# A two-layer graph network in fp32: idle products and late work at the joint, transposes in two items, pairs made one ahead, and less background in one panel's scores

## The chip, the cores and the metric

The kernel runs on one core of one Trainium2 chip. The metric is the device time of one execution in microseconds (us); less is better. A program on one core has its matmuls on TensorE (PE), its vector work on VectorE (DVE), activations and copies on ScalarE (ACT), a little vector work and the stores on GpSimd (POOL), and the loads are issued by SyncE (SP). The numbers are from the profiler's record of one execution and from the times of three runs.

## The reference

There are N = 2708 nodes with D = 1024 features, all in fp32, and a 0/1 matrix `adj` of N x N. Each of two layers normalizes its input, forms attention scores, masks them with `adj`, and adds the attended features to its input:

```python
# layer 0
h = relu(layernorm(x));  f = h @ Wf;  g = h @ Wg
e = relu(f @ g.T)
attention = softmax(where(adj > 0, e, -9e15), axis=1)
x = x + attention @ (h @ W0)
# layer 1
h = relu(layernorm(x)) @ W1
e = leaky_relu((h @ a1) + (h @ a2).T, 0.2)
attention = softmax(where(adj > 0, e, -9e15), axis=1)
x = x + relu(attention @ h)
```

(The biases are zero in this case, and are left out here.)

## The kernel before, in words

**Tiles and stages.** The nodes form tiles of 128 rows. Two tiles make a pair; there are ten pairs (`NQ`), and a last unit `LEFT` that holds what is left over: the tile `MONO` and a small one, `TINY`. The columns of the attention matrix are worked through in five panels of 576, 576, 532, 512 and 512. Large matrix products go by Strassen's scheme: seven products M1 to M7 on halves in place of eight, with sums of blocks made ahead by DVE.

The order of the stages is: M = Wg Wf' in 256 products into `M_ps` (L593), up to about 147 us; `project_q` of panel 0, to 206; then for each panel p its scores (L1409), a softmax, the aggregation and the projection by W; the projection of the next panel's q lies in between. Scores of panel 0 take 206 to 365, those of panel 3 1408 to 1541. Layer 0 ends at about 2036 to 2099 with the last panel's projection and the joint, where the first exponents of layer 1 are made; layer 1 begins with `gx` (L685) at 2099.

**Scores.** `scores` runs over the ten pairs q. For each it makes the seven products M1, M6, M5, M2, M7, M3 and M4 of 8 matmuls (1.94 us apiece in panel 0, 13.58 us for an iteration; 1.73 in panel 3). The left operand `As` of a product comes from `hs_d[q]` in DRAM, in four loads for each pair, each of two products. `hs_d[q]` holds seven transposed blocks of pair q, which `make_pairs` has made and stored. After each product DVE adds it to `m1`, `t` (`st`), `sa` or `sb`, and then `behind(rate)` lets background work run. The last product of a pair, M4, is run after M1 of the next one.

**Background.** `later` is a list of pieces of work. Each has a price in us, a fetch and a body. `behind(us)` (L207) adds `us` to a credit, bounded by twice that, and runs pieces from the list's head as long as the credit is positive. So `rate` sets how much background follows each product. `make_until(q)` (L547) runs the list's head, without regard to credit, until pair q is made. A piece's fetch is issued a few pieces ahead (`ahead`). Inside scores `nc.hold = ("vector",)` keeps DVE's instructions in the order in which they are written. SP's loads are always in written order; a load into a stream buffer waits until the buffer's last reader or store is done, and every load behind it waits too.

**make_pairs** (L434) puts for each pair, in the order 0, 1, LEFT, 2, ... 9: the two normalizations of the next pair (`put_norms`), its rows, its transposes, `dots` (two dot products with a bias vector, for pairs 0 and 1 later on) and `last`: the sums on DVE and the four stores of `hs_d[q]` by POOL. `transposes(q)` (L464) turns both tiles of a pair: 4 x 4 transposes on PE into four PSUM banks `h_ps` (L457), from which ACT copies to `hsT`; for panel 0's tiles DVE copies a part of them too. This is one piece with the price 0.5, and it takes PSUM banks. In the stage of M such a piece runs between the products.

In scores, the pairs that aren't made yet are made ahead of their use: `make_until(q + 2)` stands at each iteration's head (L1458), and the rate is 1.3 until pair 9 is made, then `rates[p]`, which is 0.8, 1.0, 0.65, 0.65 and 0.65 for the five panels (L1419).

At the end of panel 0's rows a small column `r_d` per panel is stored by POOL (L275), 512 elements of 4 bytes.

**The joint.** `rows_done` (L1587) is called with each tile of layer 0's output. For the tiles of the last panel it works directly and not through `later`. The last tile of pair 9 (`ends`) closes layer 0. `keep_on(t, n)` (L1580) issues n products whose result nobody reads, of the identity with a row tile t (`on_ps`): three on `xt[0]` (tile `x_res`) ahead of the tile's normalization, two on the normalized rows (`h_last`). Then come the dots, `raise_max` (the maximum `mx` over masked scores' terms), and `shifts1`, which turns mx over the partitions (`mx_ps`, L894), reduces it (`mcol`), and from it works out `m`, `z` and `none`; in between (`keep_on(mx[0], 1)` and `make()`) one more idle product and the first part of `pair_h` (L355), which makes sums of row blocks of h for layer 1. `pair_h` gives back its second part, `rest()`: two subtractions on DVE (`g`, 128 x 512) and the stores of the blocks M3 and M7 into `hr_d`. `rest[0]()` is called right there, held in written order.

Afterwards `weights1` (L1834) spreads shift, z and none over the partitions (`sp_ps`, L265), subtracts the shift from the first, already prepared tiles (`P`), starts the exponents, and puts pieces of 2.1 into a list `front`, which goes to the head of `later`.

Of the kernel before, what the change touches and what calls it, by code (L numbers as in the profile page):

```python
# [18 lines left out]
P = 128  # L19
# [38 lines left out]
def kernel(  # L58
# [22 lines left out]
    NH = NC // 2  # L81
# [28 lines left out]
    NQ = len(pairs)  # L110
    pair_of = {t: (t // 2, t % 2) for t in range(MONO)}
    LEFT = NQ
# [328 lines left out]
    def make_pairs():  # L441
        xs, hT = {}, {}

        def fetch(q):
            xs[q] = []
            for t in units[q]:
                xs[q].append(row_halves("x"))
                load_rows_of(t, xs[q][-1], x)

        def rows(q):  # L450
            left_h(0, *xs[q]) if q == LEFT else rows_h(q, *xs[q])

        def turned(q, k, e):
            t = units[q][k]
            ps = bank("h_ps", (P, NH, P))
            for c in range(NH):
                nc.tensor.transpose(ps[:, c, :], xs[q][k][e][:, c * P:(c + 1) * P], ident)  # L457
            for i, (s, n) in enumerate(pieces[0]):
                if s == t:
                    o = first_h[e].rearrange("p (c i) -> p c i", c=NH)[:, :, i * P:i * P + n]  # L460
                    nc.vector.tensor_copy(o, ps[:, :, :n])
            return ps

        def transposes(q):  # L464
            if q == LEFT:
                two = stream("hsl", (P, 2, NH, P))
                for e in range(2):
                    nc.scalar.copy(two[:, e], turned(q, 0, e))
                    nc.scalar.copy(tinyT[:, e], turned(q, 1, e)[:, :, :B32])
                store(hsl_d.rearrange("p e c j -> p (e c j)"), two.rearrange("p e c j -> p (e c j)"))  # L470
            else:
                ts = [stream("hsT", (P, 2, NH, P)) for _ in range(4)]
                hT[q] = ts, lambda i: ts[i // 2][:, i % 2]
                for k, e, i in ((0, 0, 0), (0, 1, 3), (1, 0, 7), (1, 1, 6)):
                    nc.scalar.copy(hT[q][1](i), turned(q, k, e))
            turned_tiles.update(units[q])

        def sums(q):
            if q == LEFT:
                return  # L480
            ts, i = hT.pop(q)
            at = {m: i(k) for k, m in enumerate(BY_SCORES)}
            add(at[M5], i(7), at[M4])
            sub(at[M6], at[M5], at[M1])
            sub(at[M7], at[M1], i(7))
            sub(at[M3], at[M2], at[M6])
            for g, t in enumerate(ts):
                store(hs_d[q][:, 2 * g:2 * g + 2].rearrange("p m c j -> p (m c j)"), t.rearrange("p m c j -> p (m c j)"))

        def dots(q, k):  # L490
            t = units[q][k]
            c = col_of[t]
            dot(r_[:, c:c + 1], xs[q][k], [vb[e][:, :W] for e in range(2)], c0)
            if t == MONO:
                nc.gpsimd.dma_start(r_[:NM, HALF:HALF + 1], r_[NM:, c:c + 1])

        def drop(q, what):
            seen.setdefault(q, set()).add(what)
            if len(seen[q]) == 3:
                xs.pop(q)  # L500

        def last(q):
            sums(q)
            drop(q, "sums")
            made.add(q)

        def bias(q, k):
            dots(q, k)
            drop(q, f"dots{k}")

        seen = {}
        def put_norms(q):
            put(2.1, lambda: normalize(xs[q][0]), lambda: fetch(q))
            put(2.1, lambda: normalize(xs[q][1]))

        put_rows = lambda q: put(0.5, lambda: rows(q))
        def put_dots(q):
            for k in range(2):
                put(1.6, lambda k=k: bias(q, k), ready=lambda: vb[0] is not None)

        todo = [0, 1, LEFT] + list(range(2, NQ))
        put_norms(todo[0])
        for i, q in enumerate(todo):
            if i + 1 < len(todo):
                put_norms(todo[i + 1])
            put_rows(q)
            put(0.5, lambda q=q: transposes(q), takes_psum=True)
            if 1 < i < 4:
                put_dots(q)
            put(2.7 if q != LEFT else 0.0, lambda q=q: last(q))  # L530
            if i >= 4:
                put_dots(q)
            if i == 1:
                put_dots(todo[0])
                put_dots(todo[1])
# [870 lines left out]
    def scores(p, B):  # L1406
# [9 lines left out]
            row_on_all(rb, r_d[p], p)  # L1416
        acc = slot("acc")
        S = [None] * NT
        rates = (0.8, 1.0, 0.65, 0.65, 0.65)  # L1419
        lefts = {}  # L1420

        def product(q, m, ps, start):
# [32 lines left out]
        left_over = None  # L1455
        for q in range(NQ):
            n = P
            make_until(q + 2)  # L1458
            rate = 1.3 if NQ - 1 not in made else rates[p]
            if q + 3 <= LEFT:  # L1460
                fetch(q + 3)
            if p == 0 and q == NQ - 2:
                ahead[0] = 2
                sums_h()
            if p in ORDERED and q in (2, 6):
                (copy_residual if q == 2 else bias_residual)(p)
            sa, sb = slot("Sa"), slot("Sb")
            S[pairs[q][0]], S[pairs[q][1]] = sa, sb
            X, Y, Z = (bank(f"s{k}") for k in "xyz")
            m1, t = slot("sm1"), slot("st")  # L1470
            product(q, M1, X, True)
            for s in (lo, hi):
                add(m1[:n, s], X[:n, :h], rb[:n, s])
            if left_over:
                left_over()
            product(q, M6, Z, True)
            add(t[:n, lo], Z[:n, :h], m1[:n, hi])
            behind(rate, True)
            product(q, M5, Y, True)
            add(t[:n, hi], Y[:n, :h], m1[:n, hi])  # L1480
            if q + 2 <= LEFT:
                convert(q + 2, p > 0)
            behind(rate, True)
            product(q, M2, X, False)
            add(sa[:n, lo], X[:n, :h], rb[:n, lo])
            if q + 2 <= LEFT:
                turn(q + 2, 0)
            behind(rate, True)
            product(q, M7, Z, False)
            add(sb[:n, hi], Z[:n, :h], t[:n, hi])  # L1490
            if q + 2 <= LEFT:
                turn(q + 2, 1)
            behind(rate, True)
            product(q, M3, Y, False)
            add(sa[:n, hi], Y[:n, :h], t[:n, lo])
            finish(q, sa, 0)
            behind(2 * rate, True)
            left_over = lambda q=q, sb=sb, Z=Z, m1=m1: last(q, sb, Z, m1)
# [88 lines left out]
    def rows_done(t, xt, fetch=None):  # L1587
# [14 lines left out]
        if panel_of[t] == NP - 1:  # L1602
            done_rows[t] = row_halves("h_last")
            ends = q == NQ - 1 and whole
            if ends:
                keep_on(xt[0], 3)
            normalize(xt, done_rows[t])
            if ends:
                keep_on(done_rows[t][1], 2)
            if whole and q == NQ - 1:  # L1610
                tc.keep_in_program_order(nc.scalar.activation(stats.tile([P, 1], FP, name="warm"), eps, AF.Exp))
            raise_it = lambda: raise_max(0, q, k, first_mask[t][:, :width[0]])
            if not whole:
                dots(1)
                raise_later.append(raise_it)
                dots0 = lambda: dots(0)
                if q == NQ - 1:
                    put(1.6, lambda: held(dots0))
                else:
                    dots0()  # L1620
            else:
                last = q == NQ - 1
                raise_later.pop()()
                dots(1)
                (held if last else call)(raise_it)
                if last:
                    put(1.6, lambda: held(dots, 0))
                else:
                    dots(0)
                rest = []  # L1630
                make = lambda: rest.append(pair_h(q, *(done_rows[s] for s in pairs[q])))
                if last:
                    got["zm"] = held(shifts1, 0, lambda: (keep_on(mx[0], 1), make()))
                else:
                    make()
                (held if last else call)(rest[0])
                put_max(1, q)
                if q == NQ - 1:
                    for m in BY_QUARTERS:
                        put_quarters(m, q // 2, later)  # L1640
                    for p in range(2, NP):
                        for s in (NQ - 2, NQ - 1):
                            put_max(p, s, lazy)
# [182 lines left out]
    def weights1(p, z, m, shift):  # L1826
# [46 lines left out]
        for i in range(len(order) + LAG):  # L1873
            mk = []
            front.append([2.1, (lambda i=i, mk=mk: mk.append(load_mask(p, *order[i])))
                          if i < len(order) and not (p == 0 and units[order[i][0]][order[i][1]] in before) else None,
                          (lambda i=i, mk=mk: go(i, mk)), False, None])
        later[:0] = front
        return S, sm

# [89 lines left out]
```

## Time and profile before

| what | us |
|---|---|
| median of 3 runs | 3032.05 (3030.42 to 3034.79) |
| the profiled execution | 3029.47 |
| its span, first to last instruction | 3027.6 |
| PE busy | 2990.7 (99% of the span) |
| DVE busy | 2052.1 (68%) |
| ACT / POOL busy | 533.6 (18%) / 496.4 (16%) |
| scores of panel 0, first matmul to last | 206 to 365 |
| scores of panel 3 | 1408 to 1541 |
| last projection of layer 0 and joint | 2036 to 2099 |

A busy share is the time in which an engine executes, its own instructions overlapping counted once. A line of the timeline gives start, duration, engine, line of the kernel, operation, output and inputs, shape and count; in brackets stands the idle time ahead of it and who ended it. A line of the waits gives total, times and the longest in us. The table by stretches of time gives for each its length, for each engine its busy time and number of instructions, and then the clock that TensorE was granted (1.00 is full speed), the share of the DMA engines and GB/s.

### The profile page before, as it was taken

Reading aid. Unit: us, or ns where it says so; the run is one execution under the profiler, and the core shown is the slowest. Engines: PE = TensorE matmul, PEld = TensorE weight load, DVE = VectorE, ACT = ScalarE, POOL = GpSimd, SP = SyncE. Lnnn points to the kernel's source line nnn. Section 1 sums busy time; section 2 is a strip of 40 time slices with the busy share of each in tenths; the row PEclk is TensorE's granted clock in tenths of the full one; section 3 lists DMA queues with packets and bytes.
Section 4 is the critical chain, followed back from the end, with each engine's and each line's share of the span. In section 5 each row is a group of like instructions: output and inputs, shape, how many; then the busy total and the mean of one; then the engine's idle time right before and its main releaser. Section 6 shows DMA issues by size and latency. Waiting matters only on the chain.

```text
span 3027.6 us, 41695 instructions
## 1 busy us (share of the span) xinstructions
PE 2990.7 (99%) x14642; PEld 2293.6 (76%) x14642; DVE 2052.1 (68%) x4670; ACT 533.6 (18%) x878; POOL 496.4 (16%) x770
## 2 busy tenths in 40 slices
PE   8999999999999999999999999999999999999999
PEld 5577777667877588876888886885767959879695
DVE  5777794545772566837974366768888768787863
ACT  4420020020210112101220111202231221212200
POOL 1421111200032100233011111131211010020201
PEclk9999999999999999999999999999999999999999
DMA  7989978887388775788957597688768768888887
GB/s 244 293 304 263 324 268 317 248 260 223 117 302 223 226 215 174 263 247 275 287 171 253 179 256 240 233 309 311 261 199 267 265 208 296 287 271 297 262 298 268
DMA packets 395008, 772.11 MB, mean 255 GB/s; under 512 B 65985, under 2 KB 208225, under 8 KB 394769
## 3 DMA queue, kind: packets, MB, share of 16 engines
q1 hardware_dynamic: 334640, 590.13, 60.1%
q0 software_dynamic: 54464, 164.78, 16.1%
q10 hardware_dynamic: 5696, 14.55, 1.4%
q8 instruction: 116, 1.90, 0.2%
q14 instruction: 92, 0.75, 0.1%
HBM read 635.37 MB, written 138.11 MB: 255 GB/s over the span
## 4 chain that ended last, share of the span: by engine, by line
PE 76%; DVE 11%; issue 6%; DMA 4%; ACT 1%; POOL 1%; SPq 1%; POOLq 0%; DVEq 0%; ACTq 0%
PE sz L1431 7%; PE gy L685 6%; PE gz L685 5%; PE gz L1120 5%; PE sx L1431 5%; PE gx L685 5%; PE sy L1431 5%; PE pz L1320 5%; PE py L1320 4%; PE px L1320 4%; PE M_ps L593 3%; PE gx L1120 3%; PE gy L1120 3%; PE gv L685 3%; PE qz L685 3%
## 5 line engine op out<-in xcount | busy, mean ns | idle before, releaser
L1431 PE MATMUL sz<-B,As 128*128 128x288 f32 (+2 forms) x1200 | 291.3, 392 | 2.2 <-DVE st L45 2.0
L1431 PEld LDWEIGHTS sz<-B,As 128*128 128x128 f32 x1200 | 227.7, 190 | 49.3 <-DVE st L45 3.2
L1431 PE MATMUL sy<-B,As 128*128 128x288 f32 (+2 forms) x800 | 200.6, 394 | 2.3 <-DVE acc L45 2.3
L1431 PE MATMUL sx<-B,As 128*128 128x288 f32 (+2 forms) x800 | 199.1, 392 | 2.1 <-DMA As<-hs_d 2.1
L685 PE MATMUL gz<-Sa,hc 128*128 128x288 f32 (+2 forms) x800 | 185.8, 392 | 0.0
L1431 PEld LDWEIGHTS sy<-B,As 128*128 128x128 f32 x800 | 152.9, 191 | 33.4 <-DVE acc L45 2.5
L1431 PEld LDWEIGHTS sx<-B,As 128*128 128x128 f32 x800 | 151.8, 190 | 34.1 <-issue 4.0
L685 PEld LDWEIGHTS gz<-Sa,hc 128*128 128x128 f32 x800 | 151.5, 190 | 32.2 <-issue 2.2
L1120 PE MATMUL gz<-quarter,hc 128*128 128x128 f32 (+2 forms) x1344 | 168.8, 279 | 3.8 <-DVE gT L45 3.7
L1120 PEld LDWEIGHTS gz<-quarter,hc 128*128 128x128 f32 x1344 | 160.6, 191 | 5.1 <-DVE gT L45 4.6
L143 POOL DMA_DIRECT2D out_dram<-x_res x164 | 80.9, 500 | 468.7 <-DVE x_res L45 459.1
L1320 PE MATMUL py<-w,ps 128*128 128x512 f32 x320 | 142.3, 593 | 0.6 <-DMA w<-in_L_gnn_W_dram 0.6
L1320 PE MATMUL pz<-w,ps 128*128 128x512 f32 x320 | 142.0, 594 | 0.0
L1320 PE MATMUL px<-w,gT 128*128 128x512 f32 x320 | 141.2, 593 | 0.0
L143 POOL DMA_DIRECT2D mk_d<-mask x55 | 35.8, 652 | 509.0 <-DVE mask L45 500.9
L1320 PEld LDWEIGHTS pz<-w,ps 128*128 128x128 f32 x320 | 60.2, 190 | 76.2 <-issue 71.9
L1320 PEld LDWEIGHTS py<-w,ps 128*128 128x128 f32 x320 | 60.4, 190 | 76.0 <-issue 73.6
L593 PE MATMUL M_ps<-wgT,wfT 128*128 128x512 f32 x256 | 112.0, 593 | 2.3 <-ACT hsT L45 1.6
L1320 PEld LDWEIGHTS px<-w,gT 128*128 128x128 f32 x320 | 60.1, 190 | 71.3 <-issue 67.8
L685 PE MATMUL gy<-T,hc 128*128 128x288 f32 (+2 forms) x480 | 111.6, 394 | 0.0
L45 ACT ACTIVATE P<-P 128x576 f32<-128x576 f32 (+3 forms) x111 | 72.1, 650 | 207.4 <-DVE P L45 207.3
L685 PEld LDWEIGHTS gy<-T,hc 128*128 128x128 f32 x480 | 91.2, 190 | 19.5
(399 smaller groups left out, 5838.3 us busy)
## 6 DMA issues: line engine op xcount, KB each, us to landing
hc<-hg_d SPq DMA_DIRECT2D x175, 512.0 KB
As<-hs_d SPq DMA_DIRECT2D x150, 512.0 KB
hc<-hr_d SPq DMA_DIRECT2D x119, 512.0 KB
hc<-hs_d SPq DMA_DIRECT2D x112, 512.0 KB
w<-wt_d SPq DMA_DIRECT2D x96, 512.0 KB
w<-in_L_gnn_W_dram SPq DMA_DIRECT2D x72, 512.0 KB
md<-md_d SPq DMA_DIRECT2D x56, 512.0 KB
adj_i<-in_adj_dram SPq DMA_DIRECT2D x200, 128.0 KB
```

Source lines behind the costliest of these rows:

```text
L45: i = f(*a, **k)
L143: nc.gpsimd.dma_start(a, b)
L593: nc.tensor.matmul(ps, wfT[a][c // NH][:, c % NH, :], wgT[b][c], start=(c == 0), stop=(c == NC - 1))
L685: nc.tensor.matmul(ps[d], left(m, k, d), right(m, k), start=(start and k == 0), stop=(k == K - 1), skip_group_check=True)
L1120: nc.tensor.matmul(ps[:, d], lhs[:, d * P:(d + 1) * P], inner_right(m, n, k), start=(start and k == 0 and d == 0), stop=(k == NK - 1), ski ...
L1320: nc.tensor.matmul(ps, left[i][m][:, k, :], w_[k], start=(start and k == 0), stop=(k == NH - 1), skip_group_check=True)
L1431: nc.tensor.matmul(ps[:n, :h], lefts[q][:, i % 2, c, :n], B[m][c // 2][:, c % 2, :h], start=(start and c == 0), stop=(c == NH - 1), skip_g ...
```

## The change

Five edits, in four places.

1. `transposes` gets a second argument k, the tile of the pair. In place of one piece of 0.5 with 16 transposes there are two pieces of 0.3 with 8 each. A tile counts as turned when its own piece is done. For LEFT all is done in the first piece.
2. In scores, `make_until(q + 2)` becomes `make_until(q + 1)`, and the rate until pair 9 is made is 0.5 for the first two iterations and 1.5 from then on, in place of 1.3.
3. The rate of panel 3's scores goes from 0.65 to 0.5.
4. At the joint, four idle products instead of three stand on `xt[0]`, and one instead of two on the normalized rows.
5. The second part of `pair_h` for the last pair, `rest`, isn't run on the spot but put into `front` as its fourth piece, with a price of 1.4.

```diff
-        def transposes(q):
-            if q == LEFT:
+        def transposes(q, k):
+            if q == LEFT and k == 1:
+                turned_tiles.update(units[q])
+            elif q == LEFT:
                 two = stream("hsl", (P, 2, NH, P))
...
             else:
-                ts = [stream("hsT", (P, 2, NH, P)) for _ in range(4)]
-                hT[q] = ts, lambda i: ts[i // 2][:, i % 2]
-                for k, e, i in ((0, 0, 0), (0, 1, 3), (1, 0, 7), (1, 1, 6)):
+                if k == 0:
+                    ts = [stream("hsT", (P, 2, NH, P)) for _ in range(4)]
+                    hT[q] = ts, lambda i: ts[i // 2][:, i % 2]
+                for e, i in ((0, 7), (1, 6)) if k else ((0, 0), (1, 3)):
                     nc.scalar.copy(hT[q][1](i), turned(q, k, e))
-            turned_tiles.update(units[q])
+                turned_tiles.add(units[q][k])
...
-            put(0.5, lambda q=q: transposes(q), takes_psum=True)
+            for k in range(2):
+                put(0.3, lambda q=q, k=k: transposes(q, k), takes_psum=True)
...
-        rates = (0.8, 1.0, 0.65, 0.65, 0.65)
+        rates = (0.8, 1.0, 0.65, 0.5, 0.65)
...
-            make_until(q + 2)
-            rate = 1.3 if NQ - 1 not in made else rates[p]
+            make_until(q + 1)
+            rate = rates[p] if NQ - 1 in made else 0.5 if q < 2 else 1.5
...
             if ends:
-                keep_on(xt[0], 3)
+                keep_on(xt[0], 4)
             normalize(xt, done_rows[t])
             if ends:
-                keep_on(done_rows[t][1], 2)
+                keep_on(done_rows[t][1], 1)
...
-                (held if last else call)(rest[0])
+                if last:
+                    got["rest"] = rest[0]
+                else:
+                    rest[0]()
...
+        if "rest" in got:
+            rest = got.pop("rest")
+            front.insert(3, [1.4, None, lambda: held(rest), False, None])
         later[:0] = front
```

## The prediction, made before the result was known

> **What bounds the kernel now.** I read the busy shares first, then the waits of PE, then the timeline around each wait that belongs to an edited line, and last SP's and POOL's queues there.
>
> ```profile
> PE 2990.7 (99%) x14642; PEld 2293.6 (76%) x14642; DVE 2052.1 (68%) x4670; ACT 533.6 (18%) x878; POOL 496.4 (16%) x770
> ```
>
> PE is the bound over the whole span. The change leaves PE's instructions as they are (five idle products before and after, all transposes kept), so time can only come from PE's waits and from its clock. PE's list of waits, with the lines that the edits touch:
>
> ```profile
> PE sy L1431 <- DVE acc L45: 2.3, 1, 2.3
> PE sx L1431 <- DMA As<-hs_d: 2.1, 1, 2.1
> PE on_ps L1583 <- ACT h_last L45: 2.1, 1, 2.1
> PE sz L1431 <- DVE st L45: 2.0, 3, 0.9
> PE M_ps L593 <- ACT hsT L45: 1.6, 1, 1.6
> ...
> PE sp_ps L265 <- DVE m L45: 1.4, 2, 0.9
> ```
>
> The other waits (4.9 at the start, 3.7 and 3.2 in L1120 and L1135) are not touched. The first two sit in the first panel's scores; PE's timeline:
>
> ```profile
> 240.75 1.91 PE L457 MATMUL h_ps<-ident,x 128*128 128x128 f32 x16
> 244.96 3.87 PE L1431 MATMUL sy<-B,As 128*128 128x288 f32 x8 [2.30 <-DVE acc L45]
> 248.67 2.10 PE L1431 MATMUL sx<-B,As 128*128 128x288 f32 x8
> ...
> 270.36 2.18 PE L1431 MATMUL sx<-B,As 128*128 128x288 f32 x8 [2.13 <-DMA As<-hs_d]
> ```
>
> The product behind the first gap took 3.87 instead of 2.10. The table by stretches says why (after PE, PEld, DVE, ACT and POOL comes the granted clock):
>
> ```profile
> 245.00:249.00 4.00, 4.00 (x10) 2.90 (x11) 2.89 (x6) 0.00 (x0) 1.59 (x3) 0.57 1.12 338
> 249.00:269.00 20.00, 19.23 (x80) 14.73 (x78) 15.71 (x42) 0.00 (x0) 1.85 (x3) 1.00 0.89 227
> ...
> 2091.50:2095.00 3.50, 3.50 (x9) 1.80 (x8) 2.63 (x10) 0.93 (x2) 1.68 (x3) 0.52 1.02 321
> ```
>
> About half clock for some 3.4 us behind the gap of 2.30, none behind the gap of 2.13. Worked out over the 3.4 us ahead of each, PE was busy 31% before the first (from 241.6 it worked until 242.66), 38% before the third, 58% ahead of the gap of 2.13. The joint of the layers, DVE's timeline:
>
> ```profile
> 2092.06 0.81 DVE L45 SCALAR_TENSOR_TENSOR mx<-maskl,f,mx 128x576 f32<-128x576 bf16 x1
> ...
> 2093.52 0.69 DVE L45 TENSOR_TENSOR g<-g,h_last 128x512 f32<-128x512 f32 x1
> 2095.03 1.07 DVE L45 TENSOR_REDUCE mcol<-mx_ps 128x1 f32<-128x128 f32 x5 [0.82 <-PE mx_ps L894]
> ...
> 2097.11 0.68 DVE L45 TENSOR_TENSOR g<-h_last,g 128x512 f32<-128x512 f32 x1
> 2097.71 0.68 DVE L45 TENSOR_TENSOR g<-h_last 128x512 f32<-128x512 f32 x1
> 2098.32 0.45 DVE L45 TENSOR_TENSOR P<-P,sp_ps 128x288 f32<-128x288 f32 x1
> ```
>
> **A. Transposes in two items, early stage.** PE's order is the same up to 147 us. What moves is ACT: its four copies of pair 0 come right behind the second product of M instead of behind LEFT's normalization, so the bank for which the M_ps product at 68.22 waited 1.64 is free. Moved with it: SP's second quartet of wg loads passes LEFT's x loads, and these rows come some 5 us later; the copies of wgT pass behind TINY's normalization to about 79 to 80, and are needed at 87. I take 1.64; bounds 1.64 and −1.0 (two m copies of the q stage that then run ahead of a transposed pair's copies, 0.5 each from ACT rows).
>
> **B. First scores: pairs one ahead, 0.5 and 1.5 for each product.** Removed if all goes well: 2.30, 2.13, and the half clock, 3.87−2.10 = 1.8; together 6.2.
> The list names DVE's acc for the 2.30, but acc was long done. SP issued the second As load of pair 2 only at 240.47, when hs_d of pair 8 had landed (POOL's store 234.88 to 240.35) and freed a buffer, and it came at about 244.7. The 2.13 is the first As of pair 4: issued at 259.96 behind eight adj loads that waited for hs_d of pair 9 (246.89 to 255.56), done at 270.19.
> After, by hand along each queue: transposes of pairs 7, 8 and 9 fall at 210, 243 and 254 instead of 210, 227 and 241. DVE has 8.1 to 8.9 us of its own in an iteration of 13.58; pair 8's norms (4.2) and sums (2.5) make 14.8 in iteration 2, dots (3.1) and sums of pair 9 (2.5) 14.5 in iteration 3. DVE is late by some 2 us there, with 0.2 to 0.5 left before its adds hold PE. Pair 8's stores then start at about 248.4, in iteration 2 to 3, where the loads are those of pairs 3 and 4:
> - second As of pair 3: needed at 256.0. Its buffer comes free with a store of pair 8: those of pairs 7 and 8 landed 4.1 to 5.8 after their issue, and the load then took 4.2 (240.47 to 244.7): 256.7 to 258.4, a wait of 0.7 to 2.4. I take 1.0.
> - first As of pair 4, behind eight adj loads: needed at 263.7. Issue at 254.1 and the two earlier stretches from adj to As of 13.4 (216.84 to 230.25) and 14.6 (255.62 to 270.2) give a wait of 4 to 5. But in both of them the column store of r_d ran:
>
> ```profile
> 224.54 0.77 POOL L275 DMA_DIRECT2D r_d<-r  x1 [8.02 <-DVE bn L45]
> ...
> 256.43 0.76 POOL L275 DMA_DIRECT2D r_d<-r  x1 [7.81 <-DVE r L45]
> ```
>
> Each took 9.2 us for 2 KB, in 512 pieces of 4 bytes. After, the second one moves to about 268, behind this load. With 9.5 to 11 for the stretch the wait is 0 to 1.5; I take 1.5. The Trainium skill, DMA: Bandwidth & Descriptors, "Rules for kernel authors", says that a strided last dimension becomes one descriptor per element, and under "Issuing engines are not separate DMA queues" that all queues run on the same 16 engines. The trace agrees with both (9.2 us for 2 KB); by these the load is the quick one, and pair 5's As (needed 277.3, done 273 to 277) inherits the store.
> Gain of B: 6.2−2.5 = 3.7; bounds 6.2 and −4.8 (both waits at their long ends, 7.4, and half clock twice, 3.6).
>
> **C. Panel 3's scores, 0.65 to 0.5.** The three waits of 0.54, 0.89 and 0.58 fall on DVE's st add, late behind background. A quarter less of it a product, 0.15 × 8 = 1.2 us an iteration, covers each. The deferred work (norms, dots, g, raises of mx) still falls within this panel's scores. DVE is busy 107.8 of 133 us there: the cover is 25 us. I take 1.5; bounds 2.0 and −0.9 (one more such wait at the panel's end).
>
> **D. Joint.** Before, two idle products at half clock stood ahead of mx_ps (PE 2093.93), though mx was ready at 2092.87. After, four run on x_res (to about 2089.5) and one on h_last (2090.98 to 2091.85), so mx_ps starts at 2092.9, done by 2093.6. The reduce then waits for g only: 2093.52+0.69 = 2094.2 instead of 2095.03, a gain of 0.83. The two g's that are deferred (2 × 0.68) no longer stand ahead of P's subtraction, 1.36 more for DVE and ACT; but gx at 2099.31 starts as the three spreads end (2098.53+0.78), so that part is slack. They then go behind the sm copy; the T that PE needs at 2118.93 was ready at 2113.8, so 1.4 is covered 3 times, and the later stores of M3 and M7 are read after 2177. The clock: the emptiest 3.4 us before mx_ps is then 56 to 61% busy, close to the 58% that was not halved; a later one, from 2092, is at 45%, between the rows of 38 and 58%. I take no halving on the path and 0.8; bounds 1.5 and −1.7 (half clock on the spreads and gx).
>
> **Sum.** 1.64+3.7+1.5+0.8 = 7.6. The profiled execution took 3029.47 (span 3027.6 and 1.87 around it), 2.6 under the median of 3032.05. By it 3021.8; against the median 3024.4, which I say.
>
> **Rivals.**
> 1. *The waits only move (same).* Stores of pair 8 and the adj stretch keep their long times: the waits in B are 2.4 and 4, with half clock once 8.2, against 6.2 removed, so B loses 2.0 (0.2 without the half clock); A, C and D give 3.9: a net gain of 1.9 to 3.7, 3028 to 3030. For it: pair 9's stores took 7.3 and more beside adj and As loads (246.89 to 254.2). Against: both stretches held r_d's store.
> 2. *Slower: the first scores run out of lead.* With q+1 a pair's hs_d is stored one iteration before its neighbours' loads, and SP is strictly in order: a late store holds adj and every As behind it. SP's waits from 206 to 365:
>
> ```profile
> SPq L139 <- DMA hs_d<-hsT: 24.5, 5, 14.6
> ```
>
> It decides when pair 8's store and the stretch behind it take over 20.5 us from 248.4, ten for the store (pair 9's last took 10.3, 248.09 to 258.35) and the rest for adj and As: then pair 4's As is 6 late, pair 5's 5, pair 3's 4, with two halvings (3.6): 18.6 against the 6.2 removed and 3.9 elsewhere, 8.5 lost: 3040.5. For it also: DVE has only 0.2 to 0.5 left, so that it starts the store late itself. Against: pair 9's stores, which met adj loads, are the exception; those of pairs 7 and 8 did not take 6.
> 3. *A and D do nothing* (a wgT wait in place of 1.64; half clock on the spreads, −1.7): 7.6−2.4−1.7 = 3.5, 3028.5.
> 4. *No clock term.* The Trainium skill, TensorE: Matmul & The Clock Gate, "Why this matters for your kernels", asks only for no idle gap over about 3 us. By it gaps of 2 us cost no clock, and rival 2's two halvings drop out, 3.6, to 3037. The trace contradicts it (0.57 behind a gap of 2.30), so the sum stays; I give the rule 0.1, within the forecast, whose time it leaves.
>
> **How the numbers follow.** A measurement can tell about 0.2%, 6.06 us: faster means under 3026.0, slower over 3038.1. The forecast has 0.50, rival 1 0.20, rival 3 0.13, rival 2 0.17. The forecast's own range is 3019.5 (A 1.64, B 6.2, C 2.0 and D 1.5, with 1.2 of the runs' spread) to 3027 (B at 1.1): a tenth of it lies above 3026. Of rivals 1 and 3, a quarter lies under it, where another part is at its best; of rival 2, 0.6 lies over 3038. Faster 0.45+0.08 = 0.53, slower 0.11, same 0.36. The range goes from the lower end, 3019.5, to 3033.5, which takes in rivals 1 and 3 and leaves out most of rival 2.
>
> **What would show it.** A: the M_ps wait of 1.6 gone, and none on wgT or wT_ps in its place. B: no wait at the sy of iteration 2, PE's clock 1.0 from 240 to 275; right if the As waits from 250 to 280 sum to 2.5, wrong if over 5 or if waits on DVE's st and acc come there. C: sz waits near zero from 1408 to 1541. D: mx_ps at 2092.9 less the shifts of A to C, reduce at g's end, gx 0.8 sooner. The prediction is wrong if pair 8's store lands after 254, or if the clock halves at the spreads.

## The result, and the profile after

The changed kernel takes 3027.36 us (median of 22 runs, 3021.77 to 3034.74), the kernel before, over the same number of runs, 3033.27 (3030.01 to 3042.34). The ratio is 0.9978, with a 95% interval of 0.9972 to 0.9984: 6.7 us faster (4.9 to 8.5). The prediction was 3024.4 against 3032.05, a ratio of 0.9975 or 7.6 us.

One profile of each kernel would not have shown this. The profiled execution after took 3029.93 us, only 0.5 more than that of before: it lies 2.6 above its median, that of before 3.8 below its own. So what follows reads the two traces stage by stage, and then the same stages in twelve more executions: one more of the changed kernel, and eleven of kernels that hold some of its edits, or vary them.

PE's waits after, those with a place in the prediction or a new one (total, times, longest, in us):

```profile
PE gy L689 <- DMA hc<-hr_d: 2.6, 1, 2.6
PE sx L1435 <- DMA As<-hs_d: 2.5, 2, 1.9
PE sy L1435 <- DMA As<-hs_d: 1.6, 1, 1.6
PE sx L1435 <- DVE sm L45: 1.5, 1, 1.5
...
PE on_ps L1587 <- ACT h_last L45: 1.2, 1, 1.2
...
PE mx_ps L898 <- DVE mx L45: 0.8, 1, 0.8
```

The wait of M_ps on hsT and the three of sz on st have gone. In the first scores, 2.30 and 2.13 us and a half clock became four waits. The wait of `sx` on `sm` at the head of panel 3's scores is new, and that of `gy` on an `hr_d` load in layer 1 has grown from 0.4 to 2.6. PE's timeline after, in the first scores:

```profile
254.67 2.18 PE L1435 MATMUL sy<-B,As 128*128 128x288 f32 x8 [1.55 <-DMA As<-hs_d]
...
263.21 2.21 PE L1435 MATMUL sx<-B,As 128*128 128x288 f32 x8 [0.54 <-DMA As<-hs_d]
265.61 4.12 PE L1435 MATMUL sz<-B,As 128*128 128x288 f32 x16 [0.20 <-DMA As<-hs_d]
...
279.40 2.18 PE L1435 MATMUL sx<-B,As 128*128 128x288 f32 x8 [1.91 <-DMA As<-hs_d]
```

They are the second load of pair 3, the first two of pair 4, and the first of pair 5, together 4.2 us. Pair 8's four stores landed between 248.4 and 252.1, ahead of the 254 that the prediction had set as its limit. The clock, in the stretches after (granted clock behind POOL's busy time):

```profile
253.00:283.00 30.00, 25.80 (x104) 19.09 (x103) 23.15 (x55) 0.95 (x2) 4.24 (x7) 1.00 1.02 270
2088.00:2091.00 3.00, 2.91 (x7) 1.30 (x7) 2.94 (x17) 0.00 (x0) 1.45 (x2) 0.50 0.82 255
2177.00:2180.20 3.20, 3.20 (x7) 2.34 (x8) 3.13 (x5) 0.00 (x0) 0.00 (x0) 0.50 1.06 394
```

It is whole through the first scores, but halved at the joint (2088.02 to 2091.43, which ends as the spreads begin), and halved once more behind the grown wait of 2.6 us. A third halved stretch, from 2412.3, lies behind the last column of the table below: from there to the last product on PE the program takes 823.0 to 823.2 us in the four profiles that have one between 2412 and 2423, and 821.4 to 821.7 in the ten others. The joint, PE and then DVE:

```profile
2087.93 1.28 PE L898 MATMUL mx_ps<-ident,mx 128*128 128x128 f32 x5 [0.81 <-DVE mx L45]
...
2092.78 0.85 PE L265 MATMUL sp_ps<-ident,none 128*128 128x128 f32 x5
2093.56 0.75 PE L689 MATMUL gx<-P,hc 128*128 128x288 f32 x2
```

```profile
2088.51 0.69 DVE L45 TENSOR_TENSOR g<-g,h_last 128x512 f32<-128x512 f32 x1
2089.12 1.07 DVE L45 TENSOR_REDUCE mcol<-mx_ps 128x1 f32<-128x128 f32 x5
...
2095.15 0.68 DVE L45 TENSOR_TENSOR g<-h_last,g 128x512 f32<-128x512 f32 x1
2095.76 0.68 DVE L45 TENSOR_TENSOR g<-h_last 128x512 f32<-128x512 f32 x1
```

The reduce follows g without a gap, as the prediction had it, and gx starts as the spreads end.

The table gives how long a stage lasted in each execution, in us, between the starts of the same two products on PE in every kernel. The marks of "scores 0" and "q of panel 1" lie up to 1.5 us behind the first product of their stage, alike in all rows. "M" is from 45.7 us of the kernel before to the end of the M products; "scores 3" is from its first product to the first of the next q, so that the new wait of 1.53 is in it; "joint" begins 0.65 us ahead of the last projection and ends at the first gx of layer 1, "layer 1" is from there to the 70th product of gy on P.

| kernel | M | scores 0 | q of panel 1 | scores 3 | joint | layer 1 |
|---|---|---|---|---|---|---|
| before | 101.74 | 160.52 | 54.59 | 133.51 | 63.13 | 100.84 |
| after | 99.84 | 159.14 | 54.59 | 132.81 | 62.36 | 104.60 |
| after, again | 99.84 | 159.82 | 54.59 | 132.59 | 62.33 | 101.84 |
| only A | 99.84 | 166.92 | 54.59 | 135.15 | 63.22 | 100.22 |
| only B | 101.74 | 158.70 | 54.59 | 134.87 | 62.20 | 101.11 |
| only the deferral | 101.74 | 167.84 | 54.59 | 133.48 | 62.21 | 101.06 |
| A, C, idle products | 99.84 | 167.32 | 54.59 | 132.46 | 62.20 | 100.46 |
| A, B, C | 99.84 | 162.52 | 54.59 | 132.46 | 62.81 | 101.05 |
| after without deferral | 99.84 | 161.41 | 54.59 | 131.38 | 62.21 | 100.79 |
| the same, again | 99.84 | 159.90 | 54.59 | 132.48 | 62.45 | 101.47 |
| deferral at price 0.0 | 99.84 | 160.49 | 54.59 | 132.32 | 62.77 | 101.14 |
| deferral at price 4.2 | 99.84 | 160.68 | 54.59 | 132.29 | 62.46 | 101.44 |
| r_d held back | 99.84 | 158.98 | 60.43 | 132.60 | 62.21 | 101.88 |
| r_d held back, no deferral | 99.84 | 158.45 | 60.98 | 131.31 | 62.22 | 100.22 |

Two columns, M and q of panel 1, hold still to 0.01 us among kernels with the same edits there, and there one trace is enough. Stages outside the table swing too: from panel 0's aggregation to panel 3's scores the 14 profiles need between 985 and 991 us, with no edit in between. The scores of panel 0 swing by 7 us between executions whose instructions up to there are the same (before, and only the deferral: 160.52 and 167.84).

### The profile page after: what moved, and what is told of

It reads as the page before. It is cut to its first block, busy times and chain, and to the rows that moved or that the text cites. A ratio compares the mean times of both kernels' runs of the same rounds, so it can differ in the third digit from the quotient of the medians.

```text
span 3027.3 us, 41726 instructions
## 1 busy us (share of the span) xinstructions
PE 2992.5 (99%) x14642; PEld 2294.8 (76%) x14642; DVE 2051.7 (68%) x4670; ACT 534.1 (18%) x878; POOL 497.1 (16%) x770
## 4 chain that ended last, share of the span: by engine, by line
PE 79%; DVE 8%; issue 6%; DMA 5%; POOL 1%; ACT 1%; SPq 0%; POOLq 0%; DVEq 0%; ACTq 0%
PE sz L1435 8%; PE gy L689 6%; PE gz L689 5%; PE sx L1435 5%; PE gz L1124 5%; PE sy L1435 5%; PE gx L689 5%; PE pz L1324 4%; PE px L1324 4%; PE py L1324 4%; PE gx L1124 3%; PE gy L1124 3%; PE M_ps L597 3%; PE gv L689 3%; PE qz L689 3%
```

## The experiments

### The deferred part of pair_h

The new wait of 2.6 us for `hr_d` looked like a cost of the deferral. Two kernels take it away, one by putting the part back and one by its price:

```diff
-                if last:
-                    got["rest"] = rest[0]
-                else:
-                    rest[0]()
+                (held if last else call)(rest[0])
...
-        if "rest" in got:
-            rest = got.pop("rest")
-            front.insert(3, [1.4, None, lambda: held(rest), False, None])
```

> The changed kernel with pair_h's second part back in its old place (idle products 4 and 1, and everything else, stay). Open is why gy in layer 1 waits 2.6 us for an hr_d load at 2177 us, where the kernel before waited 0.4. Theory 1 (the deferral shifts the background): the wait falls to 0.5 or less, the drift against the kernel before stays near -5.6 at 2200 us, and the time is 2 to 4 us under that of the changed kernel. Rival (these loads vary from execution to execution whatever the order): the wait stays at 1 to 3 us and the time stays within 1.5 us. The joint itself: the reduce still 0.8 sooner if the gain came from mx_ps alone; if the deferral gave it, gx starts 0.5 to 1.4 later.

```diff
-            front.insert(3, [1.4, None, lambda: held(rest), False, None])
+            front.insert(3, [0.0, None, lambda: held(rest), False, None])
```

> The changed kernel with the deferred part priced at 0.0 instead of 1.4 in the list of background work, so that the work behind it isn't pushed back by its credit. If the credit is the cause of the 2.6 us wait at 2177, the wait falls to 0.5 or less and the time by 2 to 4 us. If the later stores of M3 and M7 themselves are the cause, or variation between executions, the wait stays between 1 and 3 us.

Measured: without the deferral 0.9959 of before (0.9945 to 0.9972), with the price 0.0 0.9960 (0.9945 to 0.9975). PE's timeline in the profile without the deferral:

```profile
2176.80 13.36 PE L689 MATMUL gy<-P,hc 128*128 128x288 f32 x54 [0.30 <-DMA hc<-hr_d]
```

The wait is 0.30 here and under 0.2 at the price 0.0. This spoke for theory 1. The kernel before with the deferral alone, and the price trebled, were to confirm it:

```diff
-                (held if last else call)(rest[0])
+                if last:
+                    got["rest"] = rest[0]
+                else:
+                    rest[0]()
...
+        if "rest" in got:
+            rest = got.pop("rest")
+            front.insert(3, [1.4, None, lambda: held(rest), False, None])
```

> The kernel before with the deferral of pair_h's second part alone, price 1.4. If the credit is what costs the hr_d wait, gy waits 1.5 to 2.6 us there near 2180 and the kernel is 1 to 4 us slower than before (1.0003 to 1.0013); gx starts no sooner, since the spreads bound it. If the wait in the changed kernel was chance or came with the other edits, the wait is 0 to 0.4 and the time the same within 1 us.

```diff
-            front.insert(3, [1.4, None, lambda: held(rest), False, None])
+            front.insert(3, [4.2, None, lambda: held(rest), False, None])
```

> The changed kernel with the deferred part priced at 4.2 instead of 1.4. If its price pushes back the background behind it (the quarters' sums and their stores, which share the queues with the hr_d loads), three times the price gives a longer wait: 3 to 8 us near 2177, or new waits of PE on DVE or ACT in 2099 to 2200, and this stage lasts 104 to 109 us instead of 100.2 to 101.1. If the price is not the cause, the stage lasts 100 to 102.6, as with 1.4.

Alone, the deferral measures 1.0009 of before (1.0000 to 1.0018), and the wait is 0.7:

```profile
PE gy L685 <- DMA hc<-hr_d: 0.7, 1, 0.7
```

At 4.2 the kernel takes 0.9976 (0.9967 to 0.9986), and there is no wait for `hr_d` at all; the stretch lasts 101.44, not 104 to 109. So a higher price does not cost more, and theory 1 falls in that form. (At the price 0.0 the half clock fell on the spreads and on gx, from 2098.3 on, the place that the prediction gave −1.7 for; its joint and layer 1 are the longer for it.) The changed kernel as it is, and the first edit of this section once more, side by side on one chip:

> The changed kernel once more, for a second profile and a time on the same chip as the three beside it. If the deferral causes the wait for hr_d near 2177, it is again 1 us or more (in three profiles with the deferral at 1.4 it was 2.61, 1.51 and 0.68, in six without it 0 to 0.62); if it was chance it is as often below 0.6. The first scores last 158.5 to 161.5 us, panel 3's scores 131.3 to 132.8. Time 0.9978 of before within 0.001.

> The changed kernel without the deferral, once more, beside the changed kernel itself. If the deferral costs 1 to 2 us in layer 1's first stage and some half clock behind it, this kernel is 0.0004 to 0.0015 lower in its ratio, and its hr_d wait is 0 to 0.6. If not, the two ratios agree within 0.0005.

The changed kernel takes 0.9973 (0.9961 to 0.9985), without the deferral 0.9970 (0.9960 to 0.9981): the times don't tell them apart. The waits: with the deferral at 1.4, 2.61, 1.47, 1.51 (with r_d held back) and 0.68; in the eight kernels without it 0 to 0.62. The stretch (the column "layer 1") lasts 102.3 us on the mean of the first four, 100.8 of the eight, but one of the four, the profile after with its half clock, makes up half of the difference: without it the mean is 101.6, and the deferral alone (101.06) lies among the eight (100.22 to 101.47). What the trace shows of how: in the four, POOL's stores of the quarters start 62.4 us after gx and SP's loads go out at 55.3, everywhere else 61.2 to 62.2 and 54.1 to 55.1. The `hr_d` load that `gy` needs is issued 71 to 73 us after gx in all 14 and takes 8 to 11 us, with several in flight; in the four it lands 81.3 to 83.3 us after gx, in the ten others 80.3 to 81.4. Why 4.2 escapes this, and whether the 1.5 us would hold over more executions, stays open: that the deferral costs time is likely by the waits, and not shown by the times. It gained nothing at the joint, where at a whole clock the kernel with the deferral alone needs 62.21, and the one with only B, which lacks it, 62.20. No kernel here is clearly faster than the changed one; without the deferral it measured 0.9959 and 0.9970 against 0.9978 and 0.9973.

### The column stores of r_d

The prediction held r_d's column store for what made pair 4's load slow, and said that pair 5's would inherit it. It did: in the changed kernel the store went out at 265.70, and the first As of pair 5, issued at 266.59, landed at 279.27, 12.7 us later (the prediction had 273 to 277), and PE started on it at 279.40. To try it, the stores of panels 3 and 4 were made to depend on the last maximum of panel 0's scores:

```diff
         S = got["S"]
+        if p == 0:
+            late = stats.tile([P, NCOL], FP, name="late")
+            for s in range(3, NP):
+                at = slice(first_col[s], first_col[s] + F)
+                nc.vector.scalar_tensor_tensor(late[:, at], got["acc"][:, at], 0.0, r_[:, at], op0=OP.mult, op1=OP.add)
+                columns_to_row(r_d[s], s, late[:, first_col[s]:])
...
-            for s in range(1, NP):
+            for s in range(1, 3):
                 columns_to_row(r_d[s], s, r_[:, first_col[s]:])
```

> The changed kernel with the two column stores of r_d for panels 3 and 4 held back until panel 0's scores are done (four words a row are recomputed by DVE from acc times 0 plus r; the result is the same). Theory (the column store is what makes loads slow): the first As of pair 5, which came 1.9 us late after 10.5 us on the way, comes in 5 to 7 us and its wait goes below 0.3; the waits for pairs 3 and 4 (1.55, 0.54, 0.20) stay within 0.6 of what they are; the time is 1 to 2 us less. Rival (loads queue behind each other and behind pair 9's stores): the wait at pair 5 stays at 1 to 2 us.

PE's timeline with r_d held back:

```profile
256.85 3.10 PE L1435 MATMUL sy<-B,As 128*128 128x288 f32 x8 [2.95 <-DVE st L45]
...
381.37 11.18 PE L689 MATMUL qy<-qT,md 128*128 128x288 f32 x32 [2.62 <-DMA md<-md_d]
```

Behind the first of these no product of the scores waits: the first load of pair 5 takes 9.0 us (7.7 in the next kernel) and is in time, as are pair 4's. In the eight kernels with B and the store in its place this load takes 11.6 to 15.1 us. But the stores now run from 367.7, at 12 to 13 us each, while the next stage loads its `md`: a wait of 2.62 that had not been there, and half clock behind it, so that this stage lasts 60.43 in place of 54.59. The first wait, at pair 3, is 2.95, put down to DVE's add here, though the load landed within 0.05 us of the add's end (2.68, by the load, in the next kernel): larger than the 1.55 of the changed kernel, with half clock behind it, but within the 1.1 to 3.8 of the eight with the store in its place. The kernel takes 0.9977 (0.9967 to 0.9986), no less than the changed one. Both edits together:

> Both: pair_h's second part in its old place, and the two r_d stores held back. If both theories hold, 3 to 6 us less than the changed kernel, near 3023; if neither, the same time as the changed kernel within 1.5.

0.9970 (0.9959 to 0.9981), with the same picture (60.98 in the q stage), and in its list of waits

```profile
PE qy L689 <- DMA md<-md_d: 3.9, 2, 3.4
PE qz L689 <- DMA md<-md_d: 0.4, 1, 0.4
```

The store of 2 KB makes the loads beside it late in both places in which it was put: pair 5's load is quicker in both kernels without it than in all eight with it, and `md` holds up, once it is there, a stage that takes 54.59 us in all other profiles. It needs a place where no load is due. Such a kernel was not tried.

### A, B and C by themselves

A alone (the edit of `transposes` and of its `put`):

```diff
-            put(0.5, lambda q=q: transposes(q), takes_psum=True)
+            for k in range(2):
+                put(0.3, lambda q=q, k=k: transposes(q, k), takes_psum=True)
```

> The kernel before with the two-item transposes (A) alone. By the prediction the M_ps wait of 1.6 us near 68 goes and nothing else changes: -1.64 us (0.9995). Rival: with two pieces of 0.3 the pieces of the first scores fall elsewhere too, and the waits there change by more than that, by 1 us or more in either direction.

0.9999 (0.9990 to 1.0009). The M stage is 1.90 shorter, the same in all kernels with A. The time can't show 1.9 us beside what the first scores swing; they lasted 166.92 here.

B alone:

```diff
-            make_until(q + 2)
-            rate = 1.3 if NQ - 1 not in made else rates[p]
+            make_until(q + 1)
+            rate = rates[p] if NQ - 1 in made else 0.5 if q < 2 else 1.5
```

> The kernel before with the edit of the first scores (B) alone. The prediction's step gives -3.7 us (0.9988). The rival, that the waits only move, gives 0 to -1, and a profile with As waits of 4 to 6 us in 250 to 285. M_ps keeps its 1.6 us wait, panel 3 its three sz waits, the joint its idle products at half clock.

0.9992 (0.9983 to 1.0002), 2.4 us faster, with an interval from 5.2 faster to 0.6 slower. The first scores last 158.70. The opposite, A and C and the idle products without B:

```diff
-            put(0.5, lambda q=q: transposes(q), takes_psum=True)
+            for k in range(2):
+                put(0.3, lambda q=q, k=k: transposes(q, k), takes_psum=True)
...
-        rates = (0.8, 1.0, 0.65, 0.65, 0.65)
+        rates = (0.8, 1.0, 0.65, 0.5, 0.65)
...
-                keep_on(xt[0], 3)
+                keep_on(xt[0], 4)
...
-                keep_on(done_rows[t][1], 2)
+                keep_on(done_rows[t][1], 1)
```

> The kernel before with the two-item transposes (A), the rate 0.5 in panel 3's scores (C) and the idle products 4 and 1 (the one half of D), without the edit of the first scores (B) and without the deferral. In five profiles of kernels with B the waits of the first scores summed to 3.0 to 6.2 us, against 4.4 and 1.8 of half clock before. If B is worth about nothing, as these say, this kernel is as fast as the one with B and without the deferral (0.996 of before, within 0.0015). If B is worth the 3.7 us of the prediction, it is 0.1% slower than that, at 0.997 to 0.998. A, C and D alone would give 1.6+2.0+0.9 = 4.5 us, 0.9985.

0.9994 (0.9981 to 1.0007), and PE's timeline in the first scores:

```profile
244.18 3.76 PE L1435 MATMUL sy<-B,As 128*128 128x288 f32 x8 [5.31 <-DMA As<-hs_d]
254.15 2.21 PE L1435 MATMUL sx<-B,As 128*128 128x288 f32 x8 [0.39 <-DMA As<-hs_d]
271.75 3.63 PE L1435 MATMUL sx<-B,As 128*128 128x288 f32 x8 [3.75 <-DMA As<-hs_d]
```

The two waits of before are both here, at their old places, but longer, 5.31 and 3.75 where the profile of before had 2.30 and 2.13, each with half clock behind it. The waits of this kind sum to 9.5 us here, 9.1 with A alone and 8.3 with the deferral alone, against the 4.4 of before from which the prediction was made. I had expected B to be worth about nothing when I compared five profiles with B to one without; four without it now last 160.5, 166.9, 167.3 and 167.8 us, mean 165.7, and eight with it (r_d in its place) 158.7 to 162.5, mean 160.3. By this B is worth some 5 us. The time of B alone, 2.4 with its interval, allows the 3.7 of the prediction, and 5 only at its very end. The time here, 1.8 us under before where A, C and the idle products should have given 4.5, has an interval that allows both.

A, B and C, with the joint as it was (idle products 3 and 2, no deferral):

> The kernel before with A, B and C alone: the joint is as before, idle products 3 and 2 and no deferral. In eight other profiles the stretch from 2036 to the first gx of layer 1 lasted 62.2 us wherever the clock stayed whole, with 3 and 2 as with 4 and 1, and 62.4 to 63.2 where it was halved. If the idle products are worth nothing by themselves, it lasts 62.2 (63.1 if halved), and the time is that of the kernel without the deferral within 0.0007. If they are worth the 0.8 of the prediction, it lasts 63.0 at a whole clock.

0.9976 (0.9967 to 0.9985). Its joint lasted 62.81, with half clock from 2096.6 on; the whole-clock case is in other rows of the table. Of the products 3 and 2 (only B) and 4 and 1 (A, C, idle products), with and without the deferral (only the deferral; r_d held back), all four last 62.20 or 62.21 where the clock stayed whole. PE's timeline with 3 and 2 (only B):

```profile
2092.10 0.77 PE L894 MATMUL mx_ps<-ident,mx 128*128 128x128 f32 x5
...
2095.24 0.85 PE L265 MATMUL sp_ps<-ident,m 128*128 128x128 f32 x5 [1.52 <-DVE m L45]
```

and with 4 and 1 (after without the deferral):

```profile
2090.21 0.77 PE L898 MATMUL mx_ps<-ident,mx 128*128 128x128 f32 x5 [0.82 <-DVE mx L45]
...
2093.35 0.85 PE L265 MATMUL sp_ps<-ident,m 128*128 128x128 f32 x5 [1.51 <-DVE m L45]
```

From mx_ps to the first spread it is 3.14 us in both, and what follows mx_ps waits for DVE alike (1.5 us).

## Why the prediction was right, and where its steps were off

The time came within 1.1 us of the predicted gain (6.7 against 7.6 us, by the ratios). Going by the means of the table's rows with and without each edit, the parts are A 2.0, B 5.3, C 2.0, D 0.35 by its idle products and minus 1.6 by the deferral: 8.1, which lies in the interval of 4.9 to 8.5. The prediction had 1.64, 3.7, 1.5 and 0.8. That the sum came so near is in part luck: by this reckoning A, B and C brought 2.4 us more than was said, and D 2.0 less.

**A (1.64): right, a little small.** M is 1.90 shorter in every execution, and the q stage behind it 0.08 (58.62 to 58.54, first product to first product of the scores). No wait on wgT or wT_ps came in its place.

**B (3.7): right in kind, mis-sized at the term that it removes.** The step counted 6.2 us of stalls before, from one profile, and that was the mildest of four. The new stalls were 4.2 us in the profile after, where 2.5 were taken: 1.55 for pair 3 (taken 1.0, within 0.7 to 2.4), 0.74 for pair 4 (taken 1.5), and 1.91 for pair 5, for which the text named the inherited store but put no price. That pair 3 came within its range is luck too: the range rests on stores of pairs 7 and 8 that land 4.1 to 5.8 us after their issue, but in the trace of before they take 5.4 to 8.9, and pair 9's last one lands at 259.22, not 258.35; pair 8's stores after took 3.8 to 5.0. The first of its two stretches from adj to As is too short in the same way: the load lands at 233.86, not 230.25, 17.0 us and not 13.4. Taken from means, the removed term is larger by 5 us (165.7 less 160.5) and the new one by 3.5 (160.3 less 154.3, the first scores of before without their 6.2 of stalls, gives 6.0 where 2.5 was taken). The two errors cancel in the main. Rival 1 had the mechanism of the loss right, waits that move from pair 2 to pairs 3 to 5, but not its sign. The prediction's own test for B, waits on As that sum to 2.5 in 250 to 280 and not over 5, came out between in the profile after, with 4.2; in the seven others of that form it is 3.6 to 6.2, with two over the 5 that it named as wrong.

**C (1.5): 2.0.** The three waits have gone in all kernels with the edit. (The kernel adds its rate seven times an iteration, not eight, so 1.05 us less background and not 1.2, which covers each of them all the same.) A wait of 1.0 to 1.5 on `sm` at the head of these scores looks like its price in the profile after, but is there with A alone and with B alone too (both have the old rate) and missing in two kernels with the new one. So it also comes and goes without the edit; whether the edit makes it more frequent (8 of 10 profiles against 2 of 4) is not shown.

**D (0.8): the step that failed, twice.** In its first half the 0.83 was read from a joint that was at half clock. Where the clock stays whole the idle products 3 and 2 are not late, and moving one of them is worth nothing (62.20 against 62.20). What is left is the half clock: it fell on three of the five joints with 3 and 2, which then last 62.8 to 63.2, and on five of the nine with 4 and 1, which then last 62.3 to 62.8; too few to tell whether the fourth product ahead makes it rarer or cheaper. The prediction also took no half clock on this path, since the emptiest 3.4 us ahead of mx_ps would be 56 to 61% busy. Its own marks give less: from 2089.5 to 2092.9 there is only the product from 2090.98 to 2091.85, 26%. In the profile after the 3.4 us ahead of mx_ps are 40% busy, and mx_ps ran at half clock. In its second half the prediction costed the deferral at nothing, since "the later stores of M3 and M7 are read after 2177", and put DVE's work behind 1.4 us of cover. What PE waited for were not these stores but the `hr_d` loads around 2165 to 2178; that the deferral pushed them is argued from the times of the issues, and the four profiles with it do not settle it. The prediction should have looked there, since the waits of before hold this line at that very product, a cover that was already used up:

```profile
PE gy L685 <- DMA hc<-hr_d: 0.4, 1, 0.4
```

**The clock.** The prediction took the busy share of the 3.4 us ahead for what decides, and left the joint's case open between 38 and 58%. In these runs gaps of the same size fall either way. After a gap of 2.73 (without the deferral), and after one of 1.97 (the same kernel again):

```profile
280.40:283.80 3.40, 3.01 (x12) 2.12 (x13) 0.82 (x2) 0.00 (x0) 0.00 (x0) 1.00 1.03 279
```

```profile
259.00:262.40 3.40, 3.40 (x8) 2.37 (x9) 3.27 (x6) 0.00 (x0) 1.01 (x2) 0.51 1.15 274
```

The longer gap left the clock whole, the shorter one halved it. The length of a gap doesn't decide by itself.

Most of what decides can be read from the record. Within an execution the halved stretches begin whole multiples of 3.4133 us apart: in the profile after at 2088.02, 2176.77 and 2412.28, which is 26.0 and 69.0 stretches apart. So they lie on a grid, and it lies differently against the program in each execution. Cut each of the 14 profiles on its grid, from 9 us after its start to 3 us ahead of its end, and compare each stretch with the one behind it. All 23 stretches with PE busy 41% or less were followed by a halved one; of 44 between 41 and 58%, 13 were; of the more than 12 000 above that, two, both of them halved themselves. For the two gaps of before:

```profile
241.62:245.03 3.41, 1.11 (x11) 0.90 (x9) 3.31 (x9) 1.82 (x4) 0.53 (x1) 1.00 1.01 388
265.51:268.92 3.41, 2.72 (x12) 1.79 (x10) 2.27 (x9) 0.00 (x0) 1.08 (x2) 1.00 0.77 170
268.92:272.34 3.42, 1.98 (x8) 1.63 (x9) 1.35 (x2) 0.00 (x0) 0.00 (x0) 1.00 0.99 368
```

The gap of 2.30 lies in one stretch, 33% busy; the gap of 2.13 is split over two, 80 and 58% busy. The prediction's 58% is that of the last of these; the 3.4 us right ahead of the product at 270.36 were 37% busy, so the rule as the prediction words it, without the grid, would have halved the clock there as it did behind the 38% of its third case. The two gaps of the fences further up fall in the open middle, both with 42% in the stretch that counts, so this share does not tell them apart. The Trainium skill, TensorE: Matmul & The Clock Gate, "Why this matters for your kernels", asks for no idle gap over about 3 us; the runs disagree, with half clock behind 1.97 us. Rival 4 was thus rightly left out.

Rival 2 (a late store holds all of SP's loads) did not come about with B. The sizes of its waits are found without B instead: 5.31 us (A, C and the idle products) and 5.71 (only the deferral).

## What to carry to other kernels

Before a stall is priced from one profile, look whether its stage repeats: a stage that is bound by PE alone repeated here to 0.01 us, one that waits for transfers under full queues swung by 7, and the gain of an edit there is that of two means. A wait of a few tenths for a load, in a stage whose other transfers an edit moves, is a warning that its cover is gone. Where the profile shows a stretch at half clock, price an edit for both clocks: what looks like a late instruction may be only that. A gap of 2 us may or may not bring such a stretch, according to where the grid of that execution cuts it; one whose surroundings are emptier than 41% wherever it is cut always did here.

## What was not expected of the hardware

A store of 512 separate words, 2 KB, took 8 to 14 us wherever it stood in or behind the first scores, and the loads issued within some 2.5 us of it came late: 11.6 to 15.1 us for a load that took 7.7 and 9.0 with the store out of its way, or 2.6 to 4.3 us of waits and half clock in a stage that lasted 54.59 us everywhere else. The Trainium skill, DMA: Bandwidth & Descriptors, "Rules for kernel authors", says that such a store falls apart into one descriptor for each element; the time for 2 KB fits this, though the packet records do not show the 512 pieces one by one (124 packets under 512 bytes in 224.5 to 234 of before), and the runs add what it costs the others.

The half clock came in stretches of 3.41 us, or two of them in a row, in none to four places of an execution ahead of its end, and at different places in executions of the same kernel. Behind the same product each stretch cost about 1.7 us where PE was the bound (3.87 in place of 2.10 for eight products), and next to nothing at the joint after (62.36 us against 62.20, 0.16), where PE waited anyway.
